# Layer 0 of a two-layer graph transformer: second products ahead of the turn, a new pace for the attention steps, and an earlier query for the last tile

## The chip, the core and the metric

The kernel runs on one core of a Trainium2 chip. Its time is the device time of one execution in microseconds (us). Before the change the median of three runs is 1836.16 us (1835.38 to 1836.59).

## What is computed

Two transformer layers run over 2,708 nodes of width 512, with 8 heads of 64 and a hidden layer of 2,048, all in float32. Each layer is the following, and a node attends only to its neighbours in `adj` and to itself:

```
mask = adj + eye
q, k, v = h @ Wq.T + bq, h @ Wk.T + bk, h @ Wv.T + bv
scores = where(mask == 0, -1e9, q . k / 8);  attn = softmax(scores)
h1 = layer_norm(h + (attn @ v) @ Wo.T + bo)
h2 = layer_norm(h1 + relu(h1 @ W1.T + b1) @ W2.T + b2)
```

The adjacency is sparse: no node has more than 22 neighbours.

## The kernel before, in words

**Tiles and blocks.** The nodes are sorted by their number of neighbours and cut into 22 tiles of 128 rows (tile 21 has 20). `CAPS` gives the most neighbours of a row of each tile: 22 for tile 0, 14 for tile 1, 3 for tile 21. Two tiles make a block; the eleven blocks are (20,19), (18,17), (8,9), (7,10), (6,11), (5,12), (4,13), (3,14), (2,15), (1,16), (21,0), numbered 0 to 10 here. `order` is their list, so its last three tiles are 16, 21 and 0.

**Attention runs as steps beside the matmuls.** `attend` (L1748) is a generator. One step, written g.i here, takes the i-th group of one or two neighbours of each row of tile g. POOL has gathered their keys and values by indirect DMA (L1113), three steps ahead, into five buffers (`KVB`). VectorE multiplies keys by the query (L1150) and sums per head (L1156). One step later the group is weighed: ScalarE takes the exponentials (L1169) and scales one neighbour's values, head by head (L1176, eight instructions), and VectorE does the other neighbour (L1182) and adds both up (L1189). Two steps after a tile's last group come its closing sums on VectorE (L1197 to L1212), three steps after it ScalarE divides (L1220, eight instructions). Only then is the tile in `got`, and TensorE can transpose its context.

**Feed-forward sets the pace.** Each block k loops over 16 hidden chunks f of 128 columns. A chunk is four matmuls into `pf` (L1515, or L1645 in blocks 2 to 9) and a Relu on ScalarE into `ft` (L1526, L1656). In blocks 2 to 9 of layer 0 ("seven blocks", `feed_forward_by_seven`) there are two places in PSUM for `pf`. There two chunks make a pair j, VectorE forms sums of `ft` (`sums`, L1617 to L1620), and `products` (L1635) does seven matmuls instead of eight, with forms of W2 that SP reads from memory (`ask_forms`, L1602). The other blocks use `second` (L1488), two matmuls a chunk.

The order in a seven block, which every engine's queue keeps, is as follows. At f = 5 TensorE transposes the previous block's output (L1285), at f = 6 and 7 it makes keys and values of it (L620; VectorE and ScalarE copy them out in L1723 and L1728), at f = 8 POOL writes these to memory. At f = 10 the context of the next block's first tile is transposed (ScalarE copies it, L1290). At f = 11 that tile's output projection `o` runs (L620, L615) and the second tile's context is transposed; at f = 12 comes its `o`. VectorE then adds the residual and normalizes (L1447, L1450, L1269 to L1279). At f = 15 `turned` transposes both h tiles for the next block. `products(j)` runs behind chunk f = 2j + 5; products(5) thus stands behind the turn. Then follow the last pair as plain matmuls (L1665, L1669), products(6), and on VectorE the block's output (L1688 to L1695) and its norm.

**Credit.** After each chunk `advance` (L1810 on) adds a number from `PACE7[f]` (other tables for other blocks) to a credit of at most 1.5 and runs steps while it is above zero and fewer than three tiles wait in `got`. A step costs half its number of neighbours (0.5 or 1), an empty closing step 0.2:

```
credit = min(credit + more, 1.5)
while credit > 0 and len(got) < CXB:
    cost = next(ahead, None)
    ...
    credit -= cost
```

At f = 10 and f = 11 `until(g)` runs whatever steps the next block's two tiles still lack.

**Queries.** At a tile's first step `asked` fetches the next tile's query: in layer 0 POOL gathers it (L1113), in layer 1 SP reads it. Three buffers (`QB`) hold queries.

Of the kernel before, what the change touches and what calls it, by code (L numbers as in the profile page):

```python
# [25 lines left out]
NFC = FF // P  # L26
# [13 lines left out]
LAG = 3  # L40
# [11 lines left out]
    (0.0,) * 4 + (0.85,) * 8 + (0.0,) * 2 + (0.8,) * 2,  # L52
    (0.75,) * 11 + (0.0,) * 2 + (0.9,) * 3,
)
PACE7 = (0.0,) * 4 + (0.6,) + (1.3,) * 4 + (0.6,) * 2 + (0.0,) * 2 + (0.5, 0.8, 2.4)
FORMED = 1
FORMS = (3, 5, 7, 9, 11, 13, 15)
PACE = (
# [425 lines left out]
def by_edges(ctx: ExitStack, tc: tile.TileContext, x, xT, adj, layers, out, redo):  # L484
# [809 lines left out]
    class Layer:  # L1294
# [172 lines left out]
        def feed_forward(self, block, hs, hT):  # L1467

            w = sum(size(g) for g in block)
            accs = [ps_a.tile([P, DM], F32, tag=f"a{i}", name=f"a{i}") for i in range(len(block))]  # L1470
            fts = []
            apart = self.n == NL - 1 and block == blocks[-1]
            if apart:
                wide = [
                    at.tile([P, SLOTS, 2 * DM], F32, tag="kv", name="fts", bufs=KVB)
                    for _ in range(2)
                ]
                wide = [t.rearrange("p s (i w) -> p (s i) w", w=2 * P) for t in wide]

            def second(f, only=None, cols=slice(0, DM), to=None):  # L1480
                c0 = 0
                for g, a in zip(block, accs):
                    a = a if to is None else to
                    r = size(g)
                    if only not in (None, g) or r <= Q4:
                        c0 += r
                        continue
                    nc.tensor.matmul(  # L1488
                        a[:r, cols],
                        fts[f][:, c0 : c0 + r],  # L1490
                        self.w2[f // 2][:, f % 2, cols],
                        start=(f == 0),
                        stop=(f == NFC - 1),
                    )
                    c0 += r

            def quarters(f):
                c0 = 0
                for g, a in zip(block, accs):
                    r = size(g)  # L1500
                    for i in range(f - 3, f + 1) if r <= Q4 else ():
                        q = i % 4 * Q4
                        nc.tensor.matmul(
                            a[q : q + r],
                            fts[i][:, c0 : c0 + r],
                            self.w2[i // 2][:, i % 2, :],
                            start=(i < 4),
                            stop=(i >= NFC - 4),
                        )
                    c0 += r  # L1510

            for f in range(NFC):
                pf = ps_f.tile([P, DM], F32, tag="f", name="pf")
                for c in range(NC):
                    nc.tensor.matmul(  # L1515
                        pf[:, :w],
                        self.w1[f // 2][:, c, f % 2 * P : f % 2 * P + P],
                        hT[:, c, :w],
                        start=(c == 0),
                        stop=(c == NC - 1),  # L1520
                    )
                if apart:
                    ft = wide[f // 8][:, f % 8, :]
                else:
                    ft = dn.tile([P, 2 * P], F32, tag="ft", name="ft", bufs=4)
                nc.scalar.activation(ft[:, :w], pf[:, :w], AF.Relu, bias=self.b1[:, f : f + 1])  # L1526
                fts.append(ft)
                if f >= LAG and not apart:
                    second(f - LAG)
                if not apart and f % 4 == 3 and f < NFC - 1:  # L1530
                    quarters(f)
                if apart and f % 4 == 0 and f:
                    quarters(f - 1)
                yield None
            if apart:
                for f in range(4):
                    second(f, block[1], slice(0, DM // 2))
                quarters(NFC - 1)
            for g in () if apart else block:
                for f in range(NFC - LAG, NFC):  # L1540
                    second(f, g)
                    if g == block[-1] and f == NFC - LAG:
                        quarters(NFC - 1)
            zs = []
            for g, a, h in zip(block, accs, hs):
                r = size(g)
                z, st = h, None
                if apart and r > Q4:
                    st = small.tile([P, 2, 6], F32, tag="st2", name="st2", bufs=1)
                    for i in range(2):  # L1550
                        cols = slice(i * DM // 2, (i + 1) * DM // 2)
                        if i:
                            a = ps_f.tile([P, DM], F32, tag="f", name="pf")
                        for f in range(0 if i else 4, NFC):
                            second(f, g, cols, a)
                        nc.vector.tensor_tensor(z[:r, cols], a[:r, cols], h[:r, cols], ALU.add)
                        nc.vector.bn_stats(st[:r, i], z[:r, cols])
                else:
                    nc.vector.tensor_tensor(z[:r], a[:r], h[:r], ALU.add)
                    plus_rest(z[:r], a, r)  # L1560
                norm(z, r, self.g2, self.e2, st)
                if self.n == NL - 1:
                    put(out, ident_i[:r, g : g + 1], z[:r], "out")
                zs.append(z)
            yield zs
# [39 lines left out]
        def feed_forward_by_seven(self, k, block, hs, hT):  # L1605

            J, W = NFC // 2 - 1, 2 * P
# [33 lines left out]
            for f in range(NFC):  # L1641
                j = f // 2
                pf = ps_f.tile([P, DM], F32, tag="f", name="pf")
                for c in range(NC):
                    nc.tensor.matmul(  # L1645
                        pf[:, :W],
                        self.w1[j][:, c, f % 2 * P : f % 2 * P + P],
                        hT[:, c, :],
                        start=(c == 0),
                        stop=(c == NC - 1),  # L1650
                    )
                if f % 6 < 4:
                    ft = dn.tile([P, W], F32, tag="ft", name="ft", bufs=4)
                else:
                    ft = self.more_fts[f % 2]
                nc.scalar.activation(ft, pf[:, :W], AF.Relu, bias=self.b1[:, f : f + 1])  # L1656
                fts.append(ft)
                if f % 2 == 0 and j > 0:
                    sums(j - 1)
                yield None  # L1660
                if f % 2 and j > 1:
                    products(j - 2)
            for i in range(2):
                f, w = 2 * J + i, self.w2[J]
# [85 lines left out]
    def attend(n, got):  # L1750

        peak = small.tile([P, NT], F32, tag="peak", name="peak", bufs=1)
        nc.vector.memset(peak, 0.0)
        loaded = loads(n)
        steps = []
        for g in order:
            cuts = chunks_of(g)
            steps += [(g, s0, c, i, i + 1 == len(cuts)) for i, (_, s0, c) in enumerate(cuts)]
            if g == order[1]:
                steps += [None] * 3  # L1760
        steps += [None] * 3
        kv = next(loaded)
        yield 0.0
        q = asked(n, order[0])
        done = [None] * 3
        for k, step in enumerate(steps):
            if step:
                g, s0, c, i, last = step
                if i == 0:
                    while q is None:  # L1770
                        q = asked(n, g)
                        if q is None:
                            yield None
                    t, q = Tile(g, q), None
                if k > 0:
                    kv = next(loaded)
                t.weights(kv, s0, c)
                if q is None and g != order[-1]:
                    q = asked(n, order[order.index(g) + 1])
                done.append((t, kv, s0, c, last))  # L1780
            else:
                done.append(None)
            t3, t2, t1 = done[-4:-1]
            if t1:
                t1[0].weigh(*t1[1:4])
            if t2 and t2[-1]:
                t2[0].sums(peak)
            if t3 and t3[-1]:
                got[t3[0].g] = t3[0].divided()
            yield c / SLOTS if step else 0.2  # L1790
        nc.vector.tensor_reduce(flags[:, 4 + n : 5 + n], peak, AX.X, ALU.max)
        nc.vector.tensor_scalar(
            flags[:, 4 + n : 5 + n], flags[:, 4 + n : 5 + n], SAFE, None, ALU.is_le
        )
# [276 lines left out]
```

## Time and profile before

| | |
|---|---|
| median of the runs shown | 1836.16 us |
| profiled execution: own time / span | 1835.82 us / 1834.1 us |
| PE busy | 1809.1 us |
| seven blocks, mean distance of the same point in two of them | about 77 us |
| layer 0, block 0 to block 9 | about 285 to 1012 us of the span |

The span runs from the first to the last instruction; the profiled execution's own time is 1.7 us longer. A float32 matmul is recorded as two instructions, so the four matmuls of a chunk show as x8. In the view of waits, "A <- B" says that A's engine stood idle until B's instruction ended; the numbers are us in total, times, and the longest. In a timeline each line has start, length, engine, line and operation; the square bracket is the idle time ahead of it and what ended it. In the table of windows each engine's busy time stands in the order PE, PEld, DVE, ACT, POOL, then the granted TensorE clock, the DMA share and GB/s.

### The profile page before, as it was taken

How to read it: one execution, taken by the hardware profiler on the slowest of the kernel's cores; microseconds unless marked ns; L12 is line 12 of the kernel's file. 1: busy time of each engine (PE TensorE's matmuls, PEld its weight loads, DVE VectorE, ACT ScalarE, POOL GpSimd, SP SyncE). 2: the span in 40 equal slices, each digit the busy share in tenths (PEclk: the TensorE clock that was granted, in tenths of full speed). 3: DMA queues.
4: the chain of work that ended last, by engine and by line, in shares of the span. 5: the costliest groups of instructions: out<-in, count | busy, mean ns of one | idle time of the engine just before them, and what ended most of it. 6: DMA issues, size and time to landing. Idle time of an engine off the chain costs nothing.

```text
span 1834.1 us, 22527 instructions
## 1 busy us (share of the span) xinstructions
PE 1809.1 (99%) x6563; PEld 1163.0 (63%) x6563; DVE 1458.5 (80%) x2447; ACT 948.7 (52%) x3271; POOL 798.9 (44%) x745
## 2 busy tenths in 40 slices
PE   9999999999999999999999999999999999999998
PEld 4444456666677867778677644666666666666666
DVE  5987778988989889898795247887898898889853
ACT  5770435644556545564553113655665665567531
POOL 3234755534455544454440032443554554456302
PEclk9999999999999999999999999999999999999999
DMA  9987987756576575665652776845564664555300
GB/s 342 376 324 255 376 277 246 235 173 230 201 253 228 193 235 194 220 234 179 219 194 69 261 254 256 303 143 196 178 213 160 218 235 159 203 196 191 132 17 21
DMA packets 158061, 393.80 MB, mean 215 GB/s; under 512 B 17514, under 2 KB 60894, under 8 KB 157928
## 3 DMA queue, kind: packets, MB, share of 16 engines
q0 software_dynamic: 70608, 252.12, 39.9%
q1 hardware_dynamic: 77162, 118.55, 18.7%
q10 hardware_dynamic: 10158, 21.61, 3.1%
q8 instruction: 53, 0.87, 0.2%
q14 instruction: 80, 0.66, 0.1%
HBM read 338.78 MB, written 53.44 MB: 214 GB/s over the span
## 4 chain that ended last, share of the span: by engine, by line
PE 81%; DVE 10%; ACT 3%; issue 3%; DMA 2%; POOL 1%; POOLq 0%; DVEq 0%; ACTq 0%
PE pf L1515 17%; PE a L1488 16%; PE q L620 8%; PE o L620 8%; PE pf L1645 7%; PE k L620 7%; PE v L620 7%; PE c L1635 4%; PE a L1635 3%; PE tp L1285 2%; DVE sc L1156 2%; DVE kv L1150 2%; ACT kv L1176 1%; POOL rd L1275 1%; DVE acc L1189 1%
## 5 line engine op out<-in xcount | busy, mean ns | idle before, releaser
L1113 POOL DMA_INDIRECT kv<-kv_d,listed x420 | 523.5, 1246 | 294.5 <-DVE acc L1189 133.3
L1515 PE MATMUL pf<-hT,w 128*128 128x256 f32 (+1 forms) x1792 | 393.2, 367 | 0.2 <-ACT ft L1526 0.2
L1515 PEld LDWEIGHTS pf<-hT,w 128*128 128x128 f32 x1792 | 323.5, 190 | 103.3 <-issue 64.4
L1488 PE MATMUL a<-w,ft 128*128 128x512 f32 x800 | 373.1, 592 | 0.0
L1176 ACT ACTIVATE kv<-kv,p 128x64 f32<-128x64 f32 x1232 | 311.0, 335 | 5.0
L1275 POOL TENSOR_TENSOR rd<-va,mhalf 128x1 f32<-128x1 f32 (+1 forms) x88 | 80.1, 910 | 525.4 <-DVE va L1273 525.3
L1150 DVE TENSOR_TENSOR kv<-kv,q 128x1024 f32<-128x1024 f32 (+1 forms) x222 | 257.0, 1157 | 19.6 <-DMA q<-q_d,ident_i 16.5
L1156 DVE TENSOR_REDUCE sc<-kv 128x16 f32<-128x1024 f32 (+1 forms) x222 | 257.9, 1162 | 7.6
L1645 PE MATMUL pf<-hT,w 128*128 128x256 f32 x1024 | 233.2, 379 | 3.8 <-ACT ft L1656 3.8
L1189 DVE TENSOR_TENSOR acc<-acc,kv 128x1024 f32<-128x1024 f32 (+2 forms) x178 | 205.4, 1154 | 35.9 <-ACT kv L1176 21.0
L1488 PEld LDWEIGHTS a<-w,ft 128*128 128x128 f32 x800 | 150.2, 190 | 113.2 <-issue 101.3
L1645 PEld LDWEIGHTS pf<-hT,w 128*128 128x128 f32 x1024 | 193.9, 190 | 37.8 <-issue 7.9
L1526 ACT ACTIVATE ft<-pf,b 128x256 f32<-128x256 f32 (+1 forms) x208 | 94.8, 458 | 197.8 <-PE pf L1515 197.6
L1169 ACT ACTIVATE p<-sc,listed 128x8 f32<-128x8 f32 x420 | 104.0, 296 | 157.2 <-DVE sc L1156 145.4
L620 PE MATMUL o<-wo,cT 128*128 128x512 f32 x336 | 151.0, 593 | 1.0 <-ACT cT L1290 1.0
L1656 ACT ACTIVATE ft<-pf,b 128x256 f32<-128x256 f32 x96 | 44.8, 467 | 160.4 <-PE pf L1645 160.4
L1182 DVE TENSOR_TENSOR kv<-kv,p 128x512 f32<-128x512 f32 (+1 forms) x178 | 123.4, 693 | 4.0 <-ACT p L1169 4.0
L620 PEld LDWEIGHTS o<-wo,cT 128*128 128x128 f32 x336 | 63.5, 190 | 74.7 <-issue 65.5
L745 DVE MAX8 tops<-code 128x8 f32<-128x247 f32 (+2 forms) x242 | 78.8, 400 | 28.8 <-ACT code L740 28.8
L1279 DVE SCALAR_TENSOR_TENSOR h<-h,rd,ln_b 128x512 f32<-128x512 f32 (+1 forms) x88 | 66.1, 751 | 44.2 <-POOL rd L1275 44.2
L1220 ACT ACTIVATE cx<-acc,su 128x64 f32<-128x64 f32 (+1 forms) x352 | 88.2, 333 | 12.9 <-DVE su L1212 7.4
L1447 DVE TENSOR_TENSOR h<-o,xb 128x512 f32<-128x512 f32 (+1 forms) x44 | 30.3, 688 | 79.2 <-PE o L620 66.3
(231 smaller groups left out, 2325.7 us busy)
## 6 DMA issues: line engine op xcount, KB each, us to landing
aj<-in_adj SPq DMA_DIRECT2D x42, 677.0 KB, 7.0
forms<-form_d SPq DMA_DIRECT2D x168, 128.0 KB, 4.5
kv_d<-kvs ACTq DMA_DIRECT2D x21, 512.0 KB, 6.7
xg<-in_xT SPq DMA_DIRECT2D x19, 512.0 KB, 7.6
w<-in_W SPq DMA_DIRECT2D x16, 512.0 KB, 6.2
kv<-kv_d,listed POOLq DMA_INDIRECT x420, 6.2
zT_d<-zT SPq DMA_DIRECT2D x22, 256.0 KB, 5.2
xb_d<-h SPq DMA_DIRECT2D x21, 256.0 KB, 6.2
```

Of the source, the lines that this page charges most:

```text
L620: nc.tensor.matmul(o[:r], xs(c), wm[:, c, :], start=(c == 0), stop=(c == NC - 1))
L1113: return nc.gpsimd.indirect_dma_start(out=to, out_offset=None, in_=table[:, :], in_offset=bass.IndirectOffsetOnAxis(ap=s, axis=0), bounds_ ...
L1150: nc.vector.tensor_tensor(kv[:r, :c, :DM], kv[:r, :c, :DM], self.q[:r].unsqueeze(1).to_broadcast([r, c, DM]), ALU.mult,)
L1156: nc.vector.tensor_reduce(self.sc[:r, s0 : s0 + c, :], kv[:r, :c, :DM].rearrange("p s (h d) -> p s h d", d=DK), AX.X, ALU.add,)
L1169: nc.scalar.activation(p[:r, s, :], self.sc[:r, s, :], AF.Exp, bias=minus[:r, g, s : s + 1])
L1176: nc.scalar.activation(to[:, i, hd], kv[:r, i, DM + h * DK : DM + (h + 1) * DK], AF.Copy, scale=p[:r, s0 + i, h : h + 1],)
L1182: nc.vector.tensor_tensor(to[:, 0, :].rearrange("p (h d) -> p h d", d=DK), kv[:r, 0, DM:].rearrange("p (h d) -> p h d", d=DK), p[:r, s0, : ...
L1189: nc.vector.tensor_tensor(self.acc[:r, :c, :], self.acc[:r, :c, :], kv[:r, :c, DM:], ALU.add)
L1488: nc.tensor.matmul(a[:r, cols], fts[f][:, c0 : c0 + r], self.w2[f // 2][:, f % 2, cols], start=(f == 0), stop=(f == NFC - 1),)
L1515: nc.tensor.matmul(pf[:, :w], self.w1[f // 2][:, c, f % 2 * P : f % 2 * P + P], hT[:, c, :w], start=(c == 0), stop=(c == NC - 1),)
L1635: nc.tensor.matmul(to, left, right, start=start, stop=stop)
L1645: nc.tensor.matmul(pf[:, :W], self.w1[j][:, c, f % 2 * P : f % 2 * P + P], hT[:, c, :], start=(c == 0), stop=(c == NC - 1),)
```

## The change

```diff
-PACE7 = (0.0,) * 4 + (0.6,) + (1.3,) * 4 + (0.6,) * 2 + (0.0,) * 2 + (0.5, 0.8, 2.4)
+PACE7 = (0.0,) * 4 + (0.6, 1.0, 1.5, 1.5, 0.8, 0.7, 0.8, 0.0, 0.0, 0.6, 0.8, 1.4)
...
             apart = self.n == NL - 1 and block == blocks[-1]
+            ahead_of_turn = self.n == 0 and block != blocks[-1]
...
                 if f >= LAG and not apart:
                     second(f - LAG)
+                if ahead_of_turn and f == NFC - 1:
+                    second(f - LAG + 1)
...
             for g in () if apart else block:
-                for f in range(NFC - LAG, NFC):
+                for f in range(NFC - LAG + ahead_of_turn, NFC):
                     second(f, g)
-                    if g == block[-1] and f == NFC - LAG:
+                    if g == block[-1] and f == NFC - LAG + ahead_of_turn:
                         quarters(NFC - 1)
...
                 if f % 2 == 0 and j > 0:
                     sums(j - 1)
+                if f == NFC - 1:
+                    products(j - 2)
                 yield None
-                if f % 2 and j > 1:
+                if f % 2 and 1 < j < J:
                     products(j - 2)
...
-        q = asked(n, order[0])
+        q, later = asked(n, order[0]), None
...
                 if q is None and g != order[-1]:
-                    q = asked(n, order[order.index(g) + 1])
+                    q, later = later or asked(n, order[order.index(g) + 1]), None
+                    if g == order[-3]:
+                        later = asked(n, order[-1])
```

It has three parts.

1. Blocks 0 and 1 of layer 0 issue `second(13)` ahead of the turn of h (before, behind it). Seven blocks issue products(5) ahead of the turn. The number of matmuls is the same.
2. `PACE7` is new. Its sum over a block goes from 10.7 to 9.7.
3. At the first step of tile 16, the query of tile 0 is fetched right behind that of tile 21, in both layers.

The instructions on each engine are the same in number; their order in the seven blocks changes with the credit. These are the steps that fall on each chunk (c stands for an empty closing step, a dash for none):

| block | f=4 | 5 | 6 | 7 | 8 | 9 | 10 | 11 | 13 to 15 |
|---|---|---|---|---|---|---|---|---|---|
| 6 before | 14.2 | 14.3 | 2.0 | 2.1 | 2.2 2.3 | - | 2.4 | - | 2.5, 2.6 15.0 |
| 9 before | 0.6 | 0.7 | 0.8 | 0.9 | 0.10 c c | c | - | - | - |
| 4 after | 12.1 | 12.2 | 12.3 | 12.4 4.0 | 4.1 | 4.2 | 4.3 | - | 4.4, 4.5 |
| 5 after | 13.0 | 13.1 | 13.2 | 13.3 3.0 | 3.1 | - | 3.2 | - | 3.3, 3.4, 3.5 |
| 6 after | 14.0 | 14.1 | 14.2 | 14.3 2.0 | - | 2.1 | 2.2 | - | 2.3, 2.4 2.5 |
| 7 after | - | 2.6 15.0 | 15.1 | 15.2 15.3 | 1.0 | - | 1.1 | 1.2 | 1.3, 1.4, 1.5 |
| 8 after | 1.6 | 16.0 | 16.1 | 16.2 16.3 | 21.0 | 21.1 | 0.0 | - | 0.1, 0.2 0.3 |
| 9 after | - | 0.4 | 0.5 0.6 | 0.7 | 0.8 | 0.9 | 0.10 | c c c | - |

The steps at f = 11 of blocks 7 and 9 after are those that `until` runs. In both kernels the second tile of the next block is divided at the third step behind its last group. Before, that falls at f = 7 or 8 in blocks 2 to 8 and at f = 9 in block 9. After, it falls at f = 8 (block 2), 9 (3 and 4), 10 (5, 6 and 8) and 11 (7 and 9). The last chunks (f = 13 to 15) have one step less than before in blocks 2 and 4.

## The prediction

> **What bounds the kernel now.** I read the page's busy times first. Then I read the waits between block 0 and block 9 of layer 0 (285 to 1012 us), where the change acts, and the windows of this stretch and of layer 1.
>
> ```profile
> span 1834.1 us, 22527 instructions
> ...
> PE 1809.1 (99%) x6563; PEld 1163.0 (63%) x6563; DVE 1458.5 (80%) x2447; ACT 948.7 (52%) x3271; POOL 798.9 (44%) x745
> ```
> ```profile
> PE tp L1285 <- DVE h L1279: 4.6, 7, 1.6
> PE pf L1645 <- ACT ft L1656: 3.8, 3, 2.2
> PE o L615 <- ACT cT L1290: 2.4, 1, 2.4
> PE a L1635 <- DMA forms<-form_d: 0.4, 1, 0.4
> PE pf L1515 <- ACT ft L1526: 0.2, 1, 0.2
> ```
> ```profile
> 285.00:1012.00 727.00, 715.61 (x2851) 518.83 (x2850) 618.91 (x1012) 386.15 (x1441) 328.28 (x270) 1.00 0.62 205
> 1080.00:1825.00 745.00, 743.95 (x2657) 471.34 (x2655) 597.17 (x810) 408.61 (x1530) 329.15 (x297) 1.00 0.51 182
> ```
>
> TensorE is the bound, and its matmuls stay as many as they were. All that can be won lies in its idle time, 727.0 - 715.6 = 11.4 us in this stretch, and the waits name it. VectorE is 85% busy there (618.9 of 727), so anything that delays its steps can come back as a wait of TensorE. The timelines place the waits. Of the seven on h, one is at the turn of block 0 (0.62 us, at 310 us). The other six stand at f = 5, where the previous block's output is transposed (0.86, 1.65, 0.29, 0.29, 0.42, 0.44 us before blocks 2, 3, 5, 6, 8, 9). No seven block waits at its turn. The three on ft are 0.79 us in blocks 5 and 6 and 2.24 us in block 8. The one on cT is the end of attention, in block 9.
>
> **What can go.** *Products ahead of the turn.* In block 0 the wait of 0.62 us gets cover from `second(13)`, 1.72 us of matmuls: -0.6. In the seven blocks products(5) covers nothing. It costs nothing either: behind the turn 6.5 us of matmuls (L1665 at 926.2 to the end of products(6) at 932.7 in block 8) stay to hide ScalarE's copies of hT, which take 2.2 us. Its forms must arrive one turn (1.0 us) sooner; at that spacing one arrival in nine blocks was late, by 0.4 us. I take 0, with 1 us as the high end.
>
> *The earlier query.* In block 8 VectorE waits for it, ScalarE then waits for VectorE, and the Relu behind them in ScalarE's queue releases `pf` late:
>
> ```profile
> 894.76 1.22 DVE L1150 TENSOR_TENSOR kv<-kv,q 128x1024 f32<-128x1024 f32 x1 [5.41 <-DMA q<-q_d,ident_i]
> ...
> 897.27 0.49 ACT L1169 ACTIVATE p<-sc,listed 128x8 f32<-128x8 f32 x2 [5.44 <-DVE sc L1156]
> ...
> 899.72 0.45 ACT L1656 ACTIVATE ft<-pf,b 128x256 f32<-128x256 f32 x1
> 900.07 0.45 ACT L1656 ACTIVATE forms<-pf,b 128x256 f32<-128x256 f32 x1
> ...
> 900.22 1.99 PE L1645 MATMUL pf<-hT,w 128*128 128x256 f32 x8 [2.24 <-ACT ft L1656]
> ```
>
> Fetched some four steps sooner, the query is there: -2.2. On POOL the gather (1.0 us) waits for tile 1's last product, just ahead of it on VectorE; behind it stand key gathers due three steps (13 us) later: 0. In layer 1 no such wait exists, and SP's earlier read hides the same way: 0.
>
> *Steps moved.* The two 0.79 us come from two steps on f = 8 and go with them: -1.6. Blocks 2 and 4 get one step (4.3 us of VectorE) less at f = 13 to 15, so their output is normalized sooner: -1.65 and -0.29. The waits of 0.86, 0.29, 0.42 and 0.44 stay. The sum of what goes is 0.6 + 2.2 + 1.6 + 1.9 = 6.4 us (6.38 unrounded).
>
> **What comes.** The steps of a tile now end one to three chunks later, while its context is due at the same f = 11. I follow VectorE (V) and ScalarE (S) in their queues' order with rows of this trace. V: a two-neighbour step 4.32 us (946.04 to 950.36: 2.44 for product and sum, 1.9 for the weighing of the step before, 1.3 where that had one neighbour); sums of a pair 1.1; closing sums 1.55, 1.4 for short tiles. S: exponentials 0.5, scaling 2.0, division 2.0, Relu 0.45, copy of cT 1.1. One fact decides: at f = 7 S stands at the copy of the values (L1728) until TensorE has made them, so V's first weighing waits. To test this, block 6 before: by the same rules V's product of 2.2 should start at 737.7 (measured 737.46), that of 2.3 at 742.7 (742.56), and `pf` should be released at 746.4, 0.3 us later than it was:
>
> ```profile
> 746.14 1.99 PE L1645 MATMUL pf<-hT,w 128*128 128x256 f32 x8 [0.79 <-ACT ft L1656]
> ```
>
> *Block 7* (times of block 7 before; values done 810.1, second context due at 826.9). V: copy of keys to 807.5; 15.2's product and sum to 810.0; weighing only from 811.1, to 814.5, as S comes from its copy; 15.3 to 816.9 and 818.8; sums of a pair 819.9; 1.0 to 822.4 and 824.3; sums 825.4; 1.1 to 827.9; weighing of 1.0 and closing of tile 15 to 829.9. S: exponentials of 1.1 to 828.4, scaling 830.4, division 832.4. TensorE waits 832.4 - 826.9 = 5.5 us.
>
> *Block 4*, same start: 12.3 weighed to 814.5, 4.0 to 816.9, 12.4 weighed to 818.3, sums 819.4, 4.1 to 821.8, closing of tile 12 to 823.8. S, at f = 9: exponentials 822.3, scaling 824.3, division 826.3; only then the Relu of f = 10 and the copy of cT, the first piece at 827.2, due for `o` at 823.5: 3.7 us. *Blocks 5 and 6*: S has cT done at 823.0, then 0.5 + 2.0 + 2.0 = 827.5 against 826.9: 0.7 us each. *Block 8*: V's sum of 21.0 ends at 821.2, S's scaling of it at 823.7, Relu and cT to 824.6 against 823.5: 1.1 us.
>
> *Block 9.* Before, this was the end:
>
> ```profile
> 970.30 1.22 DVE L1150 TENSOR_TENSOR kv<-kv,q 128x1024 f32<-128x1024 f32 x1
> ...
> 978.25 2.02 ACT L1220 ACTIVATE cx<-acc,su 128x64 f32<-128x64 f32 x8 [2.54 <-DVE flags L1791]
> ...
> 980.84 2.28 PE L615 MATMUL o<-wo,cT 128*20 128x512 f32 x8 [2.40 <-ACT cT L1290]
> ```
>
> After, seven steps are left from f = 5 instead of five from f = 4. V is free at 946.0 in both. 0.4 runs to 950.4; sums, then the copy of keys (TensorE 952.9) to 953.7; 0.5 and 0.6, waiting for S's copy of the values at 956.3, to 965.1; copy of keys, 0.7, 0.8, 0.9 and two sums to 981.1; 0.10's product and sum to 983.6; two weighings to 987.4; closing 989.0. Division ends at 991.0, the context is due at 980.2 (without the wait shown): 10.8 us. The 2.4 us of before are gone, since tile 21's cT no longer stands behind this division: +8.4.
>
> The sum of what comes is 5.5 + 3.7 + 1.4 + 1.1 + 8.4 = 20.1 us.
>
> *The clock.* Behind the wait of 2.40 us the granted clock was 0.50 to 0.62:
>
> ```profile
> 981.00:983.00 2.00, 2.00 (x8) 0.35 (x6) 0.00 (x0) 0.64 (x3) 0.00 (x0) 0.62 0.04 8
> 983.00:984.00 1.00, 1.00 (x6) 0.95 (x6) 0.80 (x2) 0.00 (x0) 0.00 (x0) 0.50 0.00 0
> 984.00:985.00 1.00, 1.00 (x4) 0.82 (x4) 0.97 (x2) 0.79 (x4) 0.00 (x0) 0.56 0.00 0
> ```
>
> That cost 2 x 0.38 + 0.50 + 0.44 = 1.7 us; behind the wait of 2.24 us it stayed at 1.00. Block 9 pays it in both kernels. Block 7's 5.5 us is longer than either, so I add 1.7; block 4's may pay it too. The Trainium skill ("TensorE: Matmul & The Clock Gate", "Part 1: The HAM clock gate") speaks against this change here: about 3.4 us without work halves the clock until about 3.4 us of work, an estimate of 1.7 us for each of blocks 4, 7 and 9. By it the sum would be 1.7 us higher than mine; the trace has the slow clock after only 2.4 us.
>
> **Sum.** -6.4 + 20.1 + 1.7 = +15.4 us on the profiled execution's 1835.8, so 1851.2; the median of the runs shown, 1836.16, lies 0.3 us above that execution.
>
> **Rivals.** *VectorE does not lose the waits at the copies* (same). It would run its steps back to back: block 7 then waits 829.6 - 826.9 = 2.7, blocks 4, 5, 6 and 8 nothing, block 9 984.4 + 2.0 - 980.2 - 2.4 = 3.8. With -6.4 that is +0.1: 1835.9. Against it stand the 17.1 us that VectorE waits for scaling in this stretch.
> *The late division is covered* (faster). If V starts f = 8's product by 815 on block 7's scale (as before, 816.2) instead of 819.9, and tile 0's closing is done by 976, its division ends before 980.2, TensorE waits nowhere, and only the gains and the 2.4 us remain: 1835.8 - 6.4 - 2.4 = 1827. For it: from 960 to 970 us, in block 9, VectorE is busy for 6.5 us of 10 only. Against it: seven steps, sums, copies and closing are 40.4 us of VectorE's work from 944 on (7 x 4.32, 5 x 1.1, 1.3, 1.9, 1.55), so 984.4 without any wait.
> *The change does not do what it says.* The products ahead of the turn find no wait in seven blocks; this is in the forecast (0.6 us in all).
> *More slow clock, and the z waits do not shorten.* 15.4 + 1.9 + 1.7 + 1.7 (block 4, and block 9 once more after so long a wait) = 20.7: 1856.5.
>
> **How the numbers follow.** Chances: forecast 0.67, slow clock 0.13, no lost waits 0.11, covered 0.09. What this measurement can tell from no change is 0.2%, 3.7 us. The likeliest is the forecast, 1851.2. The range runs from 1837.5 (no lost waits, one more slow clock) to 1857.5 (the last rival and 1 us of late forms); it leaves the covered case and most of the one without lost waits out, under 0.2. Faster 0.09, same 0.11, slower 0.80.
>
> **What would show it.** Right: no VectorE wait on q at tile 0; no wait of TensorE at the turn of block 0; new waits of `tp` on ScalarE's division (L1220) at f = 11 in blocks 7 (about 5 us) and 9 (about 10 us), and of `o` on cT in blocks 4 and 8; a slow clock behind them. Wrong: a wait at 9's `tp` under 5 us, or none in 4 and 7; then V did not lose time at f = 7.

## The result, and the profile after

| | before | after |
|---|---|---|
| median (range, runs) | 1835.90 us (1835.38 to 1836.59, 4) | 1858.67 us (1856.20 to 1859.49, 4) |
| profiled execution: own time / span | 1835.82 / 1834.1 us | 1859.49 / 1857.8 us |
| mean granted TensorE clock | 0.997 | 0.991 |

The changed kernel is slower: ratio 1.0122, 95% interval 1.0104 to 1.0139, or +22.8 us. The forecast was 1851.2 us with a range up to 1857.5. The sign was right, the size was not.

The page of the kernel after, first its span and then the busy times:

```profile
span 1857.8 us, 22528 instructions
...
PE 1817.6 (98%) x6563; PEld 1167.4 (63%) x6563; DVE 1460.0 (79%) x2447; ACT 951.7 (51%) x3271; POOL 800.3 (43%) x745
```

The same 6,563 TensorE instructions took 8.5 us more busy time than before (1817.6 against 1809.1), and the other 15.2 us of the 23.7 by which the span grew are idle time of TensorE. TensorE's waits from block 0 to the end of attention in layer 0 (285 to 1040 us) are these (us in total, times, longest):

```profile
PE tp L1285 <- ACT cx L1220: 14.4, 2, 10.0
PE tp L1285 <- DVE h L1279: 7.1, 4, 2.2
PE o L620 <- ACT cT L1290: 5.5, 2, 3.4
```

Neither of the two waits on ScalarE's division (L1220) existed before, and all waits on ft are gone. The two waits of `o` are new as well: in block 4 a division (592.84 to 594.84) stands ahead of the copy of cT in ScalarE's queue, in block 8 the scaling of a late step (911.27 to 913.29). The wait on h did not shrink but grew, from 4.6 to 7.1 us. The timeline of TensorE in the kernel after places them (start, length, line, operation; in brackets the wait ahead and what ended it):

```profile
557.84 0.66 PE L1285 MATMUL tp<-ident,h 128*128 128x128 f32 x4 [1.86 <-DVE h L1279]
...
595.51 5.40 PE L620 MATMUL o<-wo,cT 128*128 128x512 f32 x8 [3.41 <-ACT cT L1290]
...
792.87 0.66 PE L1285 MATMUL tp<-ident,h 128*128 128x128 f32 x4 [2.20 <-DVE h L1279]
...
836.62 1.91 PE L1285 MATMUL tp<-ident,cx 128*128 128x128 f32 x4 [4.37 <-ACT cx L1220]
...
913.95 3.70 PE L620 MATMUL o<-wo,cT 128*128 128x512 f32 x8 [2.07 <-ACT cT L1290]
...
958.10 1.12 PE L1285 MATMUL tp<-ident,h 128*128 128x128 f32 x4 [2.21 <-DVE h L1279]
...
1005.08 1.91 PE L1285 MATMUL tp<-ident,cx 128*128 128x128 f32 x4 [10.00 <-ACT cx L1220]
```

In order these are block 4 at f = 5, block 4 at `o`, block 7 at f = 5, block 7 at the second context, block 8 at `o`, block 9 at f = 5 and block 9 at its context. The lengths show the clock too: eight instructions of `o` take 3.70 us at 913.95 and 5.40 us at 595.51, behind the wait of 3.41 us. The windows behind block 7's wait of 4.37 us show it directly (the third number from the end is the granted clock):

```profile
836.00:838.00 2.00, 1.38 (x3) 0.55 (x3) 1.97 (x3) 2.00 (x9) 1.70 (x2) 0.50 0.81 266
838.00:840.00 2.00, 2.00 (x6) 1.62 (x6) 1.90 (x3) 1.14 (x4) 1.70 (x2) 0.50 0.84 197
```

Late divisions and a late `o` were forecast; waits at f = 5 that grow were not.

### The profile page after: what moved, and what is told of

Same layout as the page of the kernel before. It is cut to its first block, busy times and chain, and to the rows that moved or that the text cites. A ratio compares the mean times of both kernels' runs of the same rounds, so it can differ in the third digit from the quotient of the medians.

```text
span 1857.8 us, 22528 instructions
## 1 busy us (share of the span) xinstructions
PE 1817.6 (98%) x6563; PEld 1167.4 (63%) x6563; DVE 1460.0 (79%) x2447; ACT 951.7 (51%) x3271; POOL 800.3 (43%) x745
## 4 chain that ended last, share of the span: by engine, by line
PE 82%; DVE 9%; ACT 4%; issue 2%; DMA 1%; POOL 1%; POOLq 0%; DVEq 0%; ACTq 0%
PE pf L1516 17%; PE a L1489 16%; PE pf L1648 8%; PE q L620 8%; PE o L620 7%; PE k L620 7%; PE v L620 7%; PE c L1638 4%; PE a L1638 3%; PE tp L1285 2%; DVE sc L1156 2%; DVE kv L1150 2%; ACT kv L1176 1%; DVE acc L1189 1%; ACT cx L1220 1%
## 5 line engine op out<-in xcount | busy, mean ns | idle before, releaser
L1150 DVE TENSOR_TENSOR kv<-kv,q 128x1024 f32<-128x1024 f32 (+1 forms) x222 | 256.8, 1157 | 15.0 <-DMA q<-q_d,ident_i 11.1
L1648 PE MATMUL pf<-hT,w 128*128 128x256 f32 x1024 | 232.9, 379 | 0.0
L1648 PEld LDWEIGHTS pf<-hT,w 128*128 128x128 f32 x1024 | 194.0, 190 | 33.3 <-issue 8.1
L620 PE MATMUL o<-wo,cT 128*128 128x512 f32 x336 | 152.8, 599 | 6.5 <-ACT cT L1290 6.5
L1659 ACT ACTIVATE ft<-pf,b 128x256 f32<-128x256 f32 x96 | 44.8, 467 | 152.2 <-PE pf L1648 152.2
L620 PEld LDWEIGHTS o<-wo,cT 128*128 128x128 f32 x336 | 64.0, 192 | 81.9 <-issue 65.7
L1220 ACT ACTIVATE cx<-acc,su 128x64 f32<-128x64 f32 (+1 forms) x352 | 88.2, 333 | 13.9 <-DVE su L1212 10.7
```

The source lines that it names most:

```text
L620: nc.tensor.matmul(o[:r], xs(c), wm[:, c, :], start=(c == 0), stop=(c == NC - 1))
L1150: nc.vector.tensor_tensor(kv[:r, :c, :DM], kv[:r, :c, :DM], self.q[:r].unsqueeze(1).to_broadcast([r, c, DM]), ALU.mult,)
L1220: nc.scalar.activation(cx[:r, hd], self.acc[:r, 0, hd], AF.Copy, scale=self.su[:r, h : h + 1])
L1648: nc.tensor.matmul(pf[:, :W], self.w1[j][:, c, f % 2 * P : f % 2 * P + P], hT[:, c, :], start=(c == 0), stop=(c == NC - 1),)
```

## The experiments

The theory (L in the texts on record) has three parts: the new table makes divisions late; products(5) ahead of the turn makes block outputs late; and a slow clock behind the new waits adds to both. Its rivals come run by run. In each comparison the kernel before was run beside, with medians of 1836.1 to 1836.4 us. The texts on record call the earlier query of tile 0 "the later query", after its variable `later`. In the kernels that have the lines of `second(13)`, line numbers are a few higher than before (L1638 there is L1635 before, L1648 is L1645, L1659 is L1656).

### Each part alone

**pace_alone**, the kernel before with the new table and nothing else:

```diff
-PACE7 = (0.0,) * 4 + (0.6,) + (1.3,) * 4 + (0.6,) * 2 + (0.0,) * 2 + (0.5, 0.8, 2.4)
+PACE7 = (0.0,) * 4 + (0.6, 1.0, 1.5, 1.5, 0.8, 0.7, 0.8, 0.0, 0.0, 0.6, 0.8, 1.4)
```

> The kernel before with the new PACE7 and nothing else. Theory L (late divisions come from the pace; the late outputs at f = 5 come mostly from products(5) standing ahead of the turn): new waits in blocks 4, 7, 8 and 9 of about 3.4, 4.4, 2 and 10 us as in the changed kernel, less 2.4 for the old end of attention, 5 us of slow clock behind them, less 1.6 for the two waits on ft that go and 2 for earlier outputs, and up to 2 us for tile 0's query: about +19 us, 1852 to 1857. Theory P (the pace makes the late outputs too): the changed kernel's time plus what the other parts win, 1859 to 1862. If the pace is not the cause: within 4 us of 1836.

Measured: 1855.23 us (1851.81 to 1857.58), ratio 1.0104 (1.0083 to 1.0124), +19.1 us. Its waits are the 14.3 us on divisions and the 5.5 us of `o`, as in the kernel after; the wait on h stays small, 4.8 us in all (4.6 before, 7.1 after). The table alone accounts for all of the late divisions.

**products_alone**, the kernel before with products(5) ahead of the turn in the seven blocks:

```diff
+                if f == NFC - 1:
+                    products(j - 2)
                 yield None
-                if f % 2 and j > 1:
+                if f % 2 and 1 < j < J:
                     products(j - 2)
```

> The kernel before with products(5) ahead of the turn in the seven blocks and nothing else. Theory L: the turn and with it ScalarE's eight copies of hT come 3 us later, the exponentials of the last steps stand behind these copies, VectorE waits for them and makes the block's output later by 1 to 3 us, so the waits of the transposes at f = 5 grow from 4 us to 10 to 16 us in all, some with a slow clock behind: 1842 to 1852. Theory P and the prediction: nothing is hidden and nothing is lost, 1835 to 1837.

Measured: 1848.60 us (1846.65 to 1853.88), ratio 1.0077 (1.0056 to 1.0099), +12.5 us. What the prediction priced at nothing is no small thing. TensorE's waits in this kernel, over the same stretch:

```profile
PE tp L1285 <- DVE h L1279: 14.1, 9, 2.2
PE pf L1645 <- ACT ft L1656: 3.9, 3, 2.3
PE o L615 <- ACT cT L1290: 2.4, 1, 2.4
```

The forms arrive in time, and the waits on ft and cT are those of the kernel before. Only the wait on h, the normalized output, went from 4.6 to 14.1 us.

**query_alone** and **second_alone**, the kernel before with one of the other two parts:

```diff
+                    q, later = later or asked(n, order[order.index(g) + 1]), None
+                    if g == order[-3]:
+                        later = asked(n, order[-1])
```

> The kernel before with tile 0's query asked for one tile sooner and nothing else. Theory of the prediction: VectorE's wait of 5.4 us on q goes, and with it TensorE's wait of 2.2 us in block 8; block 9's VectorE is not earlier, since its start hangs on TensorE: 1833.2 to 1834.2. Rival (another wait takes its place, because the division of tile 16 or the keys' buffers end last): 1835.4 to 1836.4.

```diff
+                if ahead_of_turn and f == NFC - 1:
+                    second(f - LAG + 1)
```

> The kernel before with second(13) ahead of the turn of h in blocks 0 and 1 and nothing else. Theory of the prediction: the wait of 0.62 us at block 0's turn goes: 1835.0 to 1835.5. Rival, as for products(5): the later copies of hT hold up ScalarE, block 1's output comes later and block 2's wait of 0.86 us at f = 5 grows by as much or more: 1836 to 1838.

Measured: the query 1831.86 us (1829.79 to 1833.95), ratio 0.9978 (0.9968 to 0.9987), -4.3 us; the waits on ft fell from 3.8 to 1.6 us, which is the 2.24 us of block 8. `second` 1834.41 us (1833.32 to 1841.38), ratio 0.9994 (0.9983 to 1.0004): not distinguishable from nothing, though the wait of block 0's turn is gone from its trace. The query gave more than its wait; the profiled spans differ by 2.9 us (1834.1 to 1831.2). Block 9's wait of 0.44 us on h is gone as well, and where the rest lies was not found.

The four parts add up to 19.1 + 12.5 - 4.3 - 1.7 = +25.6 us, against +22.8 for all of them together.

### Why products(5) costs

Nothing waits for products(5) itself. But with its seven matmuls ahead, the turn comes 3 us later in each of blocks 2 to 9, and ScalarE reaches the copies of the turned h (`hT`, L1290) before the transposes are done. ScalarE's queue is in order, and the exponentials of the steps of f = 15 stand behind those copies. The timeline of ScalarE and VectorE in the kernel after, block 6, shows it; the last line is TensorE in block 7:

```profile
772.75 2.17 ACT L1290 ACTIVATE hT<-tp,b 128x128 f32<-128x128 f32 x8 [2.98 <-PE tp L1285]
...
774.76 0.53 ACT L1169 ACTIVATE p<-sc,listed 128x8 f32<-128x8 f32 x2
775.14 0.69 DVE L1182 TENSOR_TENSOR kv<-kv,p 128x512 f32<-128x512 f32 x1 [1.70 <-ACT p L1169]
...
777.38 1.23 DVE L1189 TENSOR_TENSOR acc<-acc,kv 128x1024 f32<-128x1024 f32 x1 [1.54 <-ACT kv L1176]
...
792.87 0.66 PE L1285 MATMUL tp<-ident,h 128*128 128x128 f32 x4 [2.20 <-DVE h L1279]
```

ScalarE stood still for 2.98 us with nothing wrong but a matmul that had not come; VectorE then lost 1.70 + 1.54 = 3.2 us; and behind it on VectorE stand the block's output and norm. In without_products, the same kernel with products(5) behind the turn, the copies at this place wait for nothing and VectorE loses 0.37 us:

```profile
767.15 2.17 ACT L1290 ACTIVATE hT<-tp,b 128x128 f32<-128x128 f32 x8
...
771.78 1.23 DVE L1189 TENSOR_TENSOR acc<-acc,kv 128x1024 f32<-128x1024 f32 x1 [0.37 <-ACT kv L1176]
```

The reader should see a wait move over three engines: TensorE to ScalarE to VectorE, and back to TensorE 15 us later.

**products_steps_first** tests this. It has products(5) ahead of the turn, and moves the steps of f = 15 ahead of the turn as well, so that no exponential stands behind the copies:

```diff
+                if seven and f == NFC - 1:
+                    advance(PACE7[f])
                 if more and f == NFC - 1:
                     finish(asking)
                     hT = now.turned(blocks[k + 1], hs_next)
-                advance((PACE7 if seven else (PACE if k else PACES)[n])[f])
+                if not (seven and f == NFC - 1):
+                    advance((PACE7 if seven else (PACE if k else PACES)[n])[f])
```

> The kernel before with products(5) ahead of the turn, and the attention steps of f = 15 issued ahead of the turn too, so that their exponentials stand in front of ScalarE's copies of the turned h instead of behind them. Products(5) ahead alone took 1848.6 us. Theory L (the loss comes from exponentials that wait in ScalarE's queue behind copies which wait for TensorE): most of the 12.5 us is gone, 1836 to 1841 us, and the waits of the transposes at f = 5 for the block's output fall from 14.1 us to about 5 us. Rival (the order of the matmuls itself makes the loss, the forms or the sums being late): 1847 to 1850 us.

Measured: 1834.81 us (1832.46 to 1836.77), ratio 0.9987 (0.9977 to 0.9996). All of the 12.5 us is gone, and 1.6 us more. The wait on h is 2.0 us (14.1 without the move); one wait for a copy of hT, 0.9 us, is new. The link in the middle moves with it. These are VectorE's waits on the exponentials over 285 to 1040 us in the kernel before, in products_alone and in products_steps_first:

```profile
DVE kv L1182 <- ACT p L1169: 2.5, 3, 1.2
DVE kv L1182 <- ACT p L1169: 10.6, 9, 2.1
DVE kv L1182 <- ACT p L1169: 2.6, 3, 1.2
```

So the rival falls. What is not shown is what the move of the steps is worth by itself: no run issues the steps first and leaves products(5) behind the turn, so a small price of the new order of matmuls could hide behind a gain of the move.

**after_steps_first** makes the same move within the changed kernel.

> The changed kernel with one thing moved: the attention steps of f = 15 in the seven blocks are issued ahead of the turn instead of behind it. Theory L (within the changed kernel too, products(5) costs by the exponentials behind the turn's copies): the waits of the transposes at f = 5 on the block's output fall from 7.1 us to about 2 us and the slow clock behind two of them goes, so 1847 to 1852 us, the price of the table and the gains of the query and the turn being left. Rival (in the changed kernel the tails are short enough, the whole loss is the table's): 1857 to 1860 us.

Measured: 1850.47 us (1849.57 to 1852.38), ratio 1.0077 (1.0050 to 1.0104), 8.2 us below the kernel after. Its waits:

```profile
PE tp L1285 <- ACT cx L1220: 14.3, 2, 10.0
PE o L620 <- ACT cT L1290: 5.5, 2, 3.4
PE tp L1285 <- DVE h L1279: 0.9, 1, 0.9
PE c L1638 <- DMA forms<-form_d: 0.6, 1, 0.6
```

Beside the kernel after, the row of h fell from 7.1 to 0.9 us, and one wait of 0.6 us for a form is new. At the same place as above ScalarE now has work when it would wait (the exponentials come first, the copies at 774.01 find the transposes done):

```profile
771.56 0.49 ACT L1169 ACTIVATE p<-sc,listed 128x8 f32<-128x8 f32 x2 [1.31 <-DVE sc L1156]
...
774.01 2.14 ACT L1290 ACTIVATE hT<-tp,b 128x128 f32<-128x128 f32 x8
```

**without_products** takes the other way: the changed kernel with products(5) back behind the turn.

> The changed kernel with products(5) back behind the turn; the rest of the change stays. Theory L (the table costs 19.1 us as alone, the query and the turn give 4.3 and 1.7 us): 1847 to 1852 us, about as much as with the steps first. Rival (the parts do not add up, and products(5) is free with the new table): 1857 to 1860 us.

Measured: 1852.12 us (1849.28 to 1855.99), ratio 1.0090 (1.0059 to 1.0120), 6.6 us below the kernel after. So products(5) costs 6.6 us in the changed kernel, about half of what it costs alone. The credit fits with where it is paid: with the old table each of blocks 2 to 8 runs two steps at f = 15, behind the turn, and in products_alone each of the blocks that follow them waits (1.68 to 2.22 us, block 4 only 0.23). With the new table blocks 3, 6 and 8 still have two there and blocks 2, 4, 5 and 7 one, and in the kernel after just blocks 4, 7 and 9 wait longer than without products(5). Its waits on h are 1.3 us (0.86 in block 2, 0.41 in block 9).

One block in four kernels sums it up. From the first matmul of block 4's first chunk, the transposes are due at 10.4 us (first tile) and about 10.9 us (second). The second tile is normalized at 10.0 us in the kernel before, 11.1 in products_alone, 10.7 without_products, 12.8 after, 9.3 in after_steps_first.

### What the table costs, and where

**late_end** has the new table's shape but ends with 2.4, so that its sum is 10.7 as before and the divisions are early again (f = 7 or 8 by the credit, f = 9 in block 9, as before):

```diff
+PACE7 = (0.0,) * 4 + (0.6, 1.0, 1.5, 1.5, 0.8, 0.7, 0.8, 0.0, 0.0, 0.6, 0.8, 2.4)
```

> The kernel before with the new credit table, but 2.4 instead of 1.4 at f = 15, so that its sum over a block is 10.7 again. The steps keep the new shape (small sums early, 0.8, 0.7, 0.8 at f = 8 to 10), but the second tiles of the next blocks are divided at f = 8 or 9, as before. Theory L (it is the lateness of the division that costs): the waits of about 14.3 us on the division, 3.4 us at o and the slow clock behind them are gone, so 1834 to 1839 us. Rival (it is the new spread of the steps over the chunks, whatever the sum): 1848 to 1856 us, as with the whole new table.

Measured: 1845.54 us (1842.90 to 1846.29), ratio 1.0049 (1.0032 to 1.0066), +9.2 us: between the two. The waits on divisions are gone (`tp` none, `o` 1.3 us), as the theory says. But something else was paid, in this trace:

```profile
PE tp L1285 <- DVE h L1279: 12.4, 9, 2.2
PE o L615 <- ACT cT L1290: 2.4, 1, 2.4
PE o L620 <- ACT cT L1290: 1.3, 1, 1.3
```

By the credit, blocks 3, 4 and 7 now run a step at f = 13 that ran at f = 10 before. Steps from f = 13 on stand ahead of the block's output on VectorE: in block 5 the second tile is normalized 14.25 us behind the first matmul, where it took 11.19 us before. The timeline has the new waits at f = 5 of the blocks that follow those three: 1.13 us in block 4 (before none), 3.14 in block 5 (0.29) and 3.31 in block 8 (0.42). Block 9's wait grew too, from 0.44 to 1.67 us, though block 8 has as many steps from f = 13 on as before (one of them a chunk later). Behind the waits of 2.21 us in blocks 5 and 8 the clock was low as well, and TensorE's busy time is 1813.4 us, 4.3 more than before. So lateness of the division is not all of it: the theory was too narrow.

**early_pace** has the earlier query, second(13) ahead, products(5) behind as before, and tries the other end: one step less at f = 15, all steps as early as possible.

```diff
+PACE7 = (0.0,) * 4 + (1.6, 1.3, 1.3, 1.3, 1.0, 0.9, 0.6, 0.0, 0.0, 0.5, 0.8, 1.4)
```

> The kernel before with the later query, second(13) ahead of the turn in blocks 0 and 1, and a credit table of another kind: one step less at f = 15, and steps as early as the pace allows (1.6, 1.3, 1.3, 1.3, 1.0, 0.9, 0.6 at f = 4 to 10; 0.5, 0.8, 1.4 at f = 13 to 15; sum 10.7), so that second tiles are divided by f = 7 or 8 and the last block's at f = 8 or earlier. Theory L: no waits on divisions, fewer waits on the block's output, the query's 4.3 us and the turn's 1.7 us gained: 1824 to 1830 us. Rival (VectorE is already full at f = 4 to 8 and the copies out of PSUM come late, so that new waits of TensorE at the forms and keys take the gain): 1832 to 1842 us.

Measured: 1841.71 us (1840.81 to 1844.51), ratio 1.0038 (1.0024 to 1.0052), +5.3 us. The hope fell and the rival held:

```profile
PE k L620 <- ACT zT L1290: 10.4, 6, 2.1
PE o L620 <- ACT cT L1290: 2.6, 2, 2.1
PE k L620 <- ACT kvs L1731: 1.9, 2, 1.1
PE tp L1285 <- DVE h L1279: 1.3, 2, 0.9
```

The waits on h fell to 1.3 us, but a new first row stands above them. At f = 5 ScalarE is to copy the transposed output (`zT`) for the keys; a second step at f = 4 puts another exponential and eight more scalings ahead of it, and the keys wait. By the credit blocks 3 to 8 have two steps at f = 4, blocks 2 and 9 one, and it is in those six that the keys wait. These lines are from block 5:

```profile
641.87 2.02 ACT L1176 ACTIVATE kv<-kv,p 128x64 f32<-128x64 f32 x8
...
644.15 2.14 ACT L1290 ACTIVATE zT<-tp,bo 128x128 f32<-128x128 f32 x8
...
645.32 3.70 PE L620 MATMUL k<-wk,zT 128*128 128x512 f32 x8 [1.62 <-ACT zT L1290]
```

### The clock

**busy_in_waits** is the changed kernel with useless matmuls where TensorE stands still for a division: 4 in block 7, 11 in block 9, 3 in block 4. Their results are overwritten by the real ones; they add 18 x 0.86 = 15.5 us of work.

```diff
+        for _ in range(busy):
+            nc.tensor.matmul(o, ident, wm[:, 0, :], start=True, stop=True)
...
+            for _ in range(busy[0]):
+                nc.tensor.matmul(
+                    tp.rearrange("p c t -> p (c t)"), ident, busy[1], start=True, stop=True
+                )
```

> The changed kernel with useless matmuls added where TensorE stands still for late divisions: 4 of 128x512 ahead of the second tile's transposes in block 7, 11 in block 9, 3 ahead of the first tile's o in block 4, about 0.86 us each; their results are overwritten by the real matmuls. They fill waits and take nothing away from what the waits wait for. Theory L (behind each of these waits the granted clock falls to about 0.5 for some 4 us, which costs 1.8 to 2.4 us each): with TensorE busy the clock stays at full speed there, and the time falls by 5 to 6.5 us, to 1852 to 1854 us. Rival (the low clock has another cause, or TensorE gains nothing since something else is late behind it): 1858.5 us or a little more.

Measured: 1855.76 us (1854.63 to 1857.44), ratio 1.0110 (1.0093 to 1.0127). With 15.5 us more work it took 2.9 us less. The two ranges overlap, so the time alone would not settle it; the trace does. In windows of this kernel the clock is 1.00 behind block 4's and block 9's divisions, so the slow clock there came of TensorE standing still, and the rival falls; but the 5 to 6.5 us were too many. The page has PE at 1828.2 us; less 15.5 that is 1812.7, against 1817.6 in the kernel after, so 4.9 us went. Some 1.7 us of them are luck: behind block 7's wait of 2.20 us at f = 5, which nothing fills, the clock stayed at 1.00 in this execution. That leaves about 3.2 us for the filled waits. The clock is still low in two places: behind block 9's wait on h, and in block 7, where the transposes come singly as ScalarE divides.

```profile
836.00:838.00 2.00, 1.85 (x6) 1.40 (x7) 1.90 (x3) 1.44 (x6) 1.70 (x2) 0.65 0.75 201
838.00:840.00 2.00, 2.00 (x6) 1.55 (x6) 1.90 (x4) 0.00 (x0) 1.70 (x2) 0.50 0.75 261
```

### What is left of the change

**best** keeps the earlier query, second(13) and products(5) ahead of the turn, takes the old table, and issues the steps of f = 15 ahead of the turn. **best_pace** is the same with another table of sum 10.7:

```diff
+PACE7 = (0.0,) * 4 + (0.6, 1.3, 1.3, 1.5, 1.5, 0.9, 0.7, 0.0, 0.0, 0.5, 0.8, 1.6)
```

> The changed kernel, but with the old credit table, and with the attention steps of f = 15 issued ahead of the turn: the later query, second(13) and products(5) ahead of the turn, and no late division. The parts measured 4.3 us (query), 1.7 us (second) and 1.6 us (products with the steps first) below the kernel before, each alone. Theory L (the parts of the change are harmless or useful once the pace is the old one and no exponential stands behind the turn's copies): 1828 to 1831 us, below both kernels. Rival (the parts work on the same slack, so that they do not add up): 1831.5 to 1835 us.

> The kernel best with another table of the same sum 10.7: 0.6, 1.3, 1.3, 1.5, 1.5, 0.9, 0.7 at f = 4 to 10, and 0.5, 0.8, 1.6 at f = 13 to 15. It leaves f = 4 to 6 as light as before (what early_pace overfilled) and takes some work off f = 15; the second tiles are divided at f = 7 to 9. Theory L (each chunk has its own limit: steps at f = 5 delay the turned output that keys and values wait for, steps late in f = 7 to 10 delay divisions, steps from f = 13 on delay the block's output): within 3 us of best, 1826 to 1833 us. Rival (the old table's 7 or 8 for the division is the limit): 1836 us or more.

Measured: best 1830.22 us (1826.90 to 1832.81), ratio 0.9969 (0.9956 to 0.9983), -6.0 us, below both kernels. The parts alone give 4.3 + 1.7 + 1.6 = 7.6 us; the interval (3.1 to 8.1 us) holds that sum, and also less. Its waits (the profiled execution is the fastest of the ten, and the clock stayed at 1.00 behind the 2.4 us):

```profile
PE o L615 <- ACT cT L1290: 2.4, 1, 2.4
PE pf L1648 <- ACT ft L1659: 1.6, 2, 0.8
PE tp L1285 <- DVE h L1279: 1.3, 2, 0.9
PE pf L1648 <- ACT hT L1290: 0.9, 1, 0.9
```

best_pace took 1837.39 us (1835.99 to 1838.98), ratio 1.0000 (0.9988 to 1.0013), 7.2 us above best. The rival's time came, but not for its reason: the first row is `PE o L620 <- ACT cT L1290` with 9.7 us in four waits, and none of the four stands behind a division. By the credit this table runs more steps early, not fewer, and divides the second tiles at f = 5 to 8, not at f = 7 to 9. Block 6, its worst, shows the division ended 20 us ahead of `o`; what holds the copy of cT is the scaling of a step, which ScalarE could begin only when VectorE had summed:

```profile
729.41 2.00 ACT L1220 ACTIVATE cx<-acc,su 128x64 f32<-128x64 f32 x8
...
747.60 0.49 ACT L1169 ACTIVATE p<-sc,listed 128x8 f32<-128x8 f32 x2 [2.95 <-DVE sc L1156]
748.13 2.02 ACT L1176 ACTIVATE kv<-kv,p 128x64 f32<-128x64 f32 x8
...
751.46 1.14 ACT L1290 ACTIVATE cT<-tp,bv 128x128 f32<-128x128 f32 x4
...
751.87 5.10 PE L620 MATMUL o<-wo,cT 128*128 128x512 f32 x8 [3.48 <-ACT cT L1290]
```

In blocks 3, 4 and 7 the same order stands ahead of `o`, and the nearest division ended 7.6 us or more ahead of the copy of cT. So steps that VectorE reaches late delay `o` by standing ahead of the copy, even where the division is early.

## Why the prediction was right in sign and wrong in size

The last column is the kernel after with products(5) taken back, which is the case that the prediction in fact worked out. The measured columns are single profiled executions: the one of the kernel after is the slowest of its four (1859.49 us), the one of without_products the fastest (1849.28 us), so they lie 10.2 us apart and the medians 6.6.

| term, us | predicted | after | without_products |
|---|---|---|---|
| turn of block 0 | -0.6 | -0.6 | -0.6 |
| waits on ft (query 2.2, two steps on f = 8 1.6) | -3.8 | -3.8 | -3.8 |
| block output at f = 5 (h) | -1.9 | +3.2 | -2.7 |
| late steps: block 7 (division) | +5.5 | +4.4 | +4.4 |
| block 4 (division, at `o`) | +3.7 | +3.4 | +3.4 |
| blocks 5 and 6 | +1.4 | 0 | 0 |
| block 8 (scaling, at `o`) | +1.1 | +2.1 | +2.1 |
| block 9 (division), less the 2.4 of before | +8.4 | +7.6 | +7.6 |
| clock (growth of PE's busy time) | +1.7 | +8.5 | +4.4 |
| sum | +15.4 | +24.8 | +14.8 |
| growth of the profiled span | | +23.7 | +13.5 |

The terms are rounded. The sums of the last two columns are 1.1 and 1.3 us above the growth of the spans; waits on forms and on ft of under 0.5 us, which went, are up to 0.6 of that.

- **The step that failed** is "In the seven blocks products(5) covers nothing. It costs nothing either". Its argument looked at what follows the turn on TensorE (6.5 us of matmuls that hide the copies) and at the forms. Both hold: in the kernel after TensorE waits neither for forms nor for a copy of hT. What it left out is who else waits for the turn: ScalarE, in order, with exponentials behind it. It cost 6.6 us here and 12.5 us alone, where the prediction had 0. The high end of 1 us was drawn from the forms only, so the range lacked the mechanism and its upper end of 1857.5 fell short by 1.2 us. Without products(5) the kernel takes 1852.1 us (1849.3 to 1856.0), and the 1851.2 of the forecast lies in that. That the sum fits so well (15.4 against 14.8) is in part luck: single terms are off by up to 2.7 us, some up and some down.
- **Block outputs at f = 5.** "Blocks 2 and 4 get one step less at f = 13 to 15, so their output is normalized sooner: -1.65 and -0.29" is right without products(5), where the two waits are gone. Of the four that were to stay, 0.86 and 0.41 us (blocks 2 and 9) did, and those of blocks 6 and 8 went too. In the kernel after, products(5) brings 1.86, 2.20 and 2.21 us in blocks 4, 7 and 9 (0, 0 and 0.41 without it).
- **The late divisions** are confirmed in place and nearly in size: 4.37, 3.41 and 10.00 us against 5.5, 3.7 and 10.8. The rule that VectorE loses time at f = 7, where ScalarE stands at its copy, carried these numbers: in block 7 the closing sums of tile 15 end at 835.24 us, which on the prediction's scale (5.36 us earlier) is the 829.9 that it forecast. Part of the shortfall in blocks 7 and 9 is a matter of where the time is booked. The prediction let TensorE wait for the whole division, but ScalarE divides in eight pieces and TensorE starts behind the first ones; the four transposes then take 1.91 us, waiting between them, where four that wait for nothing take 1.12 us at the same low clock (958.10 above). So 0.8 us of each of these two waits stands in TensorE's busy time, in the row of the clock; with it the two waits are 5.2 and 10.8 us. The rule gave 0.7 us too much in blocks 5 and 6, where nothing waits, and 1 us too little in block 8. The rivals "does not lose the waits" (2.7 and 3.8 us in blocks 7 and 9) and "is covered" fall.
- **The clock** was under-sized. I charged 1.7 us for block 7 alone. Of the 8.5 us, 4.4 are there without products(5): blocks 4 and 9 pay too, as the fourth rival and the estimate from the Trainium skill ("TensorE: Matmul & The Clock Gate", "Part 1: The HAM clock gate") had it. (Of the 8.5 and of the 4.4 us, 1.6 belong to the divisions, as said above.) The other 4.1 us come with products(5) in this execution: two of its waits (2.20 and 2.21 us) are followed by windows at 0.51 to 0.64. In products_alone three of the four waits on h of that length had no low clock behind them, so this part is not a fixed price. The page's 3.4 us without work is longer than those waits, so here the measurement decides.
- **The query and the turn of block 0** are confirmed in the trace: no wait on ft remains and none at the turn. The query alone gives 4.3 us, 2 us more than forecast; the gain at the turn is too small to tell from nothing in the time.

In sum the table and products(5) cost 19.1 and 12.5 us alone, by different mechanisms, and only the first was forecast. The query's gain of 4.3 us is real but small beside them; the 1.7 us of `second(13)` cannot be told from nothing.

## What to carry to other kernels

Before calling a moved block of matmuls free, ask of every engine that consumes the result behind it what stands in that engine's in-order queue after the consumer; 3 us of matmuls in each of eight blocks, moved ahead of a transpose, cost 12.5 us, and moving the queued work ahead of the copy took all of it back. A pace table for side work on a full engine has a limit at each end: too late and the next block's context is late, too much just ahead of f = 11 and the copy of that context is late, too much behind the turn and this block's output is late, too early and the copies for the keys are late; each table tried here took one of these waits away and made another. And take the slow clock into the sum: 1.7 us for each stretch of it, behind every new wait of 2.8 us or more, and as a matter of chance behind waits from 2.1 us on.

## What the hardware showed that was not expected

The granted clock fell in pieces of one size. Added up over windows of 1 us from block 0 to the end of attention in layer 0, each low stretch took 1.70 to 1.71 us of full speed away, which is some 3.4 us at 0.50, or two or three times as much: 3.42 us around block 7's wait of 4.37 us in the kernel after, 5.12 us around block 9's of 10.00 us.

The clock does not go by the length of the wait alone. In the profiles of all fourteen kernels it fell at every wait of 2.78 us or more (fourteen of them). At waits of up to 2.12 us it fell only where a second wait stood within 3 us: late_end's 0.93 and 1.10 us, each next to one of 2.21 us, and busy_in_waits' 0.94 and 0.15 us among transposes that came singly. Of the 22 waits of 2.13 to 2.42 us it fell at 13 and stayed at 1.00 at 9. What TensorE does around them does not decide it alone either. Block 9's wait of 2.21 us at f = 5, between the same transposes, ended at half clock in the kernel after and in busy_in_waits, and at full clock in products_alone and pace_alone. Between full matmuls 2.28 us brought the low clock in products_alone, and 2.24 us before did not. What else decides, these runs do not show; a single profile with such a wait can be 1.7 us slower or faster by it.

Block 9's wait in the kernel after, then in products_alone:

```profile
958.00:960.00 2.00, 1.90 (x7) 1.72 (x8) 1.86 (x9) 0.75 (x3) 1.70 (x2) 0.51 0.07 21
958.00:960.00 2.00, 2.00 (x11) 1.74 (x11) 1.93 (x4) 0.30 (x2) 1.70 (x2) 1.00 0.93 259
```

Block 7's wait of 2.20 us in the kernel after, then in busy_in_waits:

```profile
794.00:796.00 2.00, 2.00 (x7) 1.56 (x6) 1.90 (x6) 1.97 (x9) 1.64 (x2) 0.55 0.68 198
793.00:795.00 2.00, 2.00 (x12) 1.82 (x12) 1.86 (x8) 1.45 (x6) 1.70 (x2) 1.00 0.19 35
```
